# Query and key projections by heads side by side on the array, and scores on four row groups

## The chip, the cores and the metric

The kernel runs on one core of a Trainium2 chip. The metric is the device time of one execution in microseconds, the median of several runs. A core has five engines that run side by side and wait for each other by semaphores: TensorE (PE, matmuls from SBUF into PSUM, with a separate path PEld that loads the stationary operand), VectorE (DVE), ScalarE (ACT), GpSimd (POOL) and SyncE (SP, which here issues the DMA transfers). Each engine takes its instructions in the order in which they stand in its queue. TensorE can be used as one array of 128 rows by 128 columns or as smaller tiles: an operand that starts at partition 0, 32, 64 or 96 picks a row group, and the partitions of the output pick a column group.

## The reference

Input and output are 32 images of 56 x 56 pixels with 96 channels, in float32. Two layers follow each other; each adds a mixing part and a feed-forward part to the running value.

```python
# layer 0: attention in windows of 7 x 7 pixels, 3 heads of 32 channels
qkv = roll(ln(x)) @ w_qkv + b_qkv
att = einsum('bhwid,bhwjd->bhwij', q, k) * 96**-0.5 + pos_bias   # last row of windows: mask added
out = einsum('bhwij,bhwjd->bhwid', softmax(att), v) @ w_out + b_out
x = x + roll_back(out)
x = x + ffn(ln(x))            # 96 -> 384 -> 96, operands rounded to fp8 (5, 2), relu
# layer 1: a linear recurrence along the width, gated
x = x + ((sigmoid(h @ W_gate) * ssm_scan(h @ W_expand)) @ W_out)   # h: two layer norms of x
x = x + ffn(ln(x))
```

The change concerns q, k and the scores of layer 0 only: for each window of 49 pixels and each of three heads, the 49 x 49 products of keys and queries, scaled, with the position bias added.

## The kernel before

**Blocks.** The work is cut into 128 blocks: 32 images times 4 blocks of 14 image rows. A block has 784 pixels, kept as seven groups of 112 pixels on the partitions (`xb`), and is 16 windows of 7 x 7. The recurrence of layer 1 runs over whole images, as products with a Toeplitz matrix (`SC0` to `SC5`, line 802), once in four blocks.

**Steps and the table.** A block passes through some 90 named steps, each of which gives a few instructions to one engine. The table `PIPELINED` lists all steps with a lag each, `name:lag`. In iteration t the loop goes through the table from left to right and emits each step for block t - lag. The order in which the steps are emitted is kept on every engine. So the table alone decides what stands behind what in each queue; blocks of different age are interleaved within one iteration. Both tables reach from lag 0 to lag 11.

The steps that matter here, in the order in which one block meets them, with their engine:

- `LD` loads the block (SP). `sa`, `pa`, `na`, `ta`, `ea`: the first layer norm. Statistics (DVE), the power -0.5 (POOL), the scaling (DVE), the transpose (PE), and the copy into `xw` (ACT), with 96 channels and a row of ones on the partitions and the 784 pixels, ordered by windows, along the free dimension. The letters s, p, n, t, e mean the same with f (feed-forward of layer 0), e (layer 1) and g (feed-forward of layer 1).
- `q`, `k` (line 519, PE) project, `eq`, `ek` (line 531, ACT) copy to `qT`, `kT`: 96 channels on the partitions, three heads of 32 each, 784 pixels along the free dimension. `v`, `ev` do so for the values (lines 538 and 549).
- `sc` (line 561, PE): the scores of 16 windows and 3 heads, 48 products over 32 rows, 64 columns wide. `st0`, `st1`, `st2` (line 572, DVE) scale one head each and add the bias, from PSUM to `pT`; `ex0` to `ex2` (ACT) take the exponential.
- `av` (line 622, PE) multiplies by the values, `rc` (DVE) normalises, `tro`, `eo` transpose (PE, ACT), `pr` projects (PE), `ad` (line 489, DVE) adds to `xb`.
- `hf0` to `hf2` (line 690, PE), `xf` (line 702, ACT), `rf` (line 708, DVE), `cf` (line 714, DVE, and POOL for the middle one), `yf` (line 724, PE), `zf` (ACT), `bf` (DVE), `kf` (line 746, POOL): the feed-forward of layer 0. With g in place of f: that of layer 1.
- `xe` (ACT), `r0` (POOL): the input of layer 1 to `xs`. `pu0` to `pu3` (lines 778 and 779, PE): gate and expansion; `th` and `uc` (ACT) take them out of PSUM. `SC`, `GA` (line 817, DVE): recurrence and gating. `gt0`, `gt1`, `eg0`, `eg1`: transpose (PE, ACT). `so` (line 856, PE), `as` (line 489, DVE): output projection and addition. `ST` stores (SP).

**PSUM.** All products go to one pool of four buffers of two banks (`banks`), so a step on PE can start only when a buffer is free, that is, when the engine that takes its old content out is done with it.

**What `q`, `k` and `sc` do on the array.** `q` and `k` each take 128 rows and 96 columns and two products of 392 pixels. `sc` uses row group h for head h, so three of the four row groups, and the two column halves for even and odd windows. It fills two buffers, `sab` (heads 0 and 1, a bank each) and `sc` (head 2).

Of the kernel before, what the change touches and what calls it, by code (L numbers as in the profile page):

```python
# [8 lines left out]
F32 = mybir.dt.float32  # L9
# [4 lines left out]
ALU = mybir.AluOpType  # L14
# [9 lines left out]
C = 96  # L24
# [3 lines left out]
NH = 3  # L28
HD = 32
# [8 lines left out]
NBLK = 4  # L38
NRP = NBLK * G
NTOK = G * TP  # L40
NPAIR = 8
W2 = WS * WS
OVER = 64 - W2
HALF = NPAIR * W2
MASKED = -1.0e30
LNC_EPS = 1e-6
LNT_EPS = 1e-5
SSM_EPS = 1e-3
QSCALE = float(C) ** -0.5
# [3 lines left out]


PIPELINED = (
    "pu0:4 SC5:8 bg:10 xf0:3 pu2:4 xf2:3 pu3:4 pg:9 ng:9 th0:4 sa:1 uc0:4 GA5:8 ex2:2 ex0:2 th2:4 "
    "rf2:3 hf1:3 rf0:3 pu1:4 uc2:4 tg:9 th3:4 uc3:4 xf1:3 uc1:4 av:2 pa:1 gt1:8 cf2:3 cf0:3 rf1:3 "
    "kg:10 rc:2 th1:4 SC3:7 eg:9 hg1:9 eg1:8 cf1:3 na:1 yf:3 xg1:9 zf:3 GA3:7 tro:2 bf:3 eo:2 hg2:9 "
    "kf:3 xg2:9 rg1:9 rg2:9 SC1:7 gt0:8 GA1:7 cg2:9 ST:11 hg0:9 eg0:8 pr:2 xg0:9 LD:0 ad:2 ta:1 ea:1 "
    "sf:2 se:3 SC4:7 pf:2 so:8 GA4:7 as:8 q:1 pe:3 nf:2 eq:1 v:1 cg1:9 ne:3 ev:1 SC2:7 rg0:9 k:1 "  # L60
    "cg0:9 ek:1 tf:2 sg:8 ef:2 SC0:7 GA2:7 GA0:7 te:3 sc:1 xe:3 st1:1 r0:3 st2:1 st0:1 yg:9 ex1:1 "
    "zg:9 hf0:2 hf2:2 "
)

IN_TURN = (
# [10 lines left out]
def kernel(  # L76
# [27 lines left out]
    nc = tc.nc  # L104
# [3 lines left out]
    const = ctx.enter_context(tc.tile_pool(name="const", bufs=1))  # L108
# [8 lines left out]
    def banks(name):  # L117

        return psum.tile([128, 2, 512], F32, tag="ps", name=name)


    def block_dmas(i, t, xb):

        img, blk = i // NBLK, i % NBLK
        for wr in range(2):
            h0 = 2 * WS * blk + wr * WS + SH
            for a0, a1, r0 in ((0, min(WS, HW - h0), h0), (min(WS, HW - h0), WS, 0)):
                if a0 < a1:
                    rows = t[img, r0 : r0 + a1 - a0].rearrange("a w c -> w a c")
                    p0 = wr * HW  # L130

                    for w0, w1, src in ((0, 48, SH), (48, HW - SH, 48 + SH), (HW - SH, HW, 0)):
                        yield xb[p0 + w0 : p0 + w1, a0:a1, :], rows[src : src + w1 - w0]
# [5 lines left out]
    def zeros(size, name):  # L139
        t = const.tile([128, size], F32, name=name)  # L140
        nc.gpsimd.memset(t, 0.0)
        return t

    wqkv = zeros(3 * C, "wqkv")
# [87 lines left out]
    n = 1  # L232
# [63 lines left out]

    nc.vector.memset(mask[:, cut:W2], MASKED)
    nc.vector.memset(low[:, 0:cut], MASKED)
    for par in range(2):
        half = mask[par * 64 : par * 64 + 64, :]  # L300
# [3 lines left out]
        half = low[par * 64 : par * 64 + 64, :]  # L304
# [23 lines left out]
    b1T = const.tile([128, W2], F32, name="bias1T")  # L328
    nc.vector.memset(b1T, MASKED)
    for par in range(2):  # L330
# [4 lines left out]
    bias = [const.tile([128, NPAIR, W2], F32, name=f"bias_{n}") for n in range(2)]  # L335
# [49 lines left out]
    xws, vs, gTs, xqs = [], [], [], []  # L385
    for n in range(2):
# [10 lines left out]
        v = const.tile([128, NPAIR * NH, HD + 1], F32, name=f"v_{n}")  # L397
# [1 line left out]
        vs.append(v)  # L399
    ot = const.tile([128, G, 2 * NPAIR, WS], F32, name="ot")  # L400
    nc.vector.memset(ot[C:], 1.0)
    qT = const.tile([C, NTOK + OVER], F32, name="qT")
    nc.vector.memset(qT[:, NTOK:], 0.0)
    kT = const.tile([C, NTOK + OVER], F32, name="kT")
    nc.vector.memset(kT[:, NTOK:], 0.0)
    pT = const.tile([128, NH, HALF + OVER], F32, name="pT")
    nc.vector.memset(pT[:, :, HALF:], 1.0)
    xs = const.tile([128, G, 3, RS], F32, name="xs")
# [4 lines left out]
    held = {}  # L413

    def steps(*names):


        def enter(f):
            if len(names) == 1:
                step[names[0]] = f  # L420
            else:
                for k, n in enumerate(names):
                    step[n] = lambda i, k=k: f(i, k)
            return f

        return enter
# [66 lines left out]
    @steps("LD")  # L493
    def _(i):
        xb = xpool.tile([TP, G, C], F32, tag="xb", name=f"xb_{i}")
        for dst, src in block_dmas(i, x, xb):
            nc.sync.dma_start(dst, src)
        xtiles[i] = xb
# [15 lines left out]

    @steps("q", "k")
    def _(i, n):
        pq = banks(f"qk_{i}_{n}")
        for half in range(2):
            nc.tensor.matmul(  # L519
                pq[0:C, half, 0:HALF],  # L520
                wqkv[:, n * C : (n + 1) * C],
                xws[i % 2][:, half * HALF : (half + 1) * HALF],
                start=True,
                stop=True,
            )
        held["qk", i, n] = pq

    @steps("eq", "ek")
    def _(i, n):
        dst = (qT, kT)[n][:, 0:NTOK].rearrange("c (h t) -> c h t", h=2)  # L530
        nc.scalar.copy(dst, held.pop(("qk", i, n))[0:C, :, 0:HALF])  # L531

    @steps("v")
    def _(i):
# [17 lines left out]
        )  # L552

    def scores(i, stat, mov):
        pab, pc = banks(f"sab_{i}"), banks(f"sc_{i}")
        dst = [pab[:, 0], pab[:, 1], pc[:, 0]]
        for w in range(2 * NPAIR):
            p0, n0 = (w % 2) * 64, (w // 2) * W2
            for h in range(NH):
                hp = slice(h * HD, (h + 1) * HD)  # L560
                nc.tensor.matmul(
                    dst[h][p0 : p0 + 64, n0 : n0 + W2],
                    stat[hp, w * W2 : w * W2 + 64],
                    mov[hp, w * W2 : (w + 1) * W2],
                    start=True,
                    stop=True,
                )
        return [d[:, 0:HALF] for d in dst]

    def scaled(dst, i, ps):  # L570
        bt = bias[i % NBLK == NBLK - 1].rearrange("p w q -> p (w q)")
        nc.vector.scalar_tensor_tensor(dst, ps, QSCALE, bt, op0=ALU.mult, op1=ALU.add)  # L572


    @steps("sc")
    def _(i):
        held["s", i] = scores(i, kT, qT)

    @steps("st0", "st1", "st2")
    def _(i, h):  # L580
        scaled(pT[:, h, 0:HALF], i, held["s", i][h])

    @steps("ex0", "ex1", "ex2")
    def _(i, h):
# [2 lines left out]
    @steps("any")  # L587
    def _(i):

        for h, ps in enumerate(scores(i, qT, kT)):  # L590
            pr = one.tile([128, 8 * C], F32, tag="an", name=f"pr_{i}_{h}")
            nc.vector.memset(pr[:, HALF : HALF + OVER], 0.0)
            pa = pr[:, 0:HALF]
            p3 = pa.rearrange("p (w k) -> p w k", k=W2)
            scaled(pa, i, ps)
            mx = two.tile([128, NPAIR], F32, tag="mx", name=f"mx_{i}_{h}")
            nc.vector.tensor_reduce(mx, p3, op=ALU.max, axis=AX.X)
            nc.vector.tensor_tensor(p3, p3, mx[:, :, None].to_broadcast([128, NPAIR, W2]), ALU.subtract)
            nc.scalar.activation(pa, pa, AF.Exp)

            pp = banks(f"pp_{i}_{h}")
            for w in range(2 * NPAIR):
                p0, n0 = (w % 2) * 64, (w // 2) * W2
                nc.tensor.matmul(
                    pp[p0 : p0 + 64, 0, n0 : n0 + W2], pr[:, n0 : n0 + 64], ident[:, p0 : p0 + W2], start=True, stop=True
                )
            nc.scalar.copy(pT[:, h, 0:HALF], pp[:, 0, 0:HALF])
# [256 lines left out]
    def pipeline(table):  # L864
        entries = [(n, int(lag)) for n, lag in (e.split(":") for e in table.split())]
        gates = min(lag for n, lag in entries if n[0:2] == "th")
        for t in range(nblocks + 1 + max(lag for _, lag in entries)):
            if t == min(1, gates):
                load_toep()
            if t == gates:  # L870
                turn_toep()
            for name, lag in entries:
                i = t - lag
                if name[0:2] in ("SC", "GA"):
                    if i % NBLK == 0 and 0 <= i < nblocks:
                        step[name](i // NBLK)
                elif 0 <= i < nblocks:
                    step[name](i)
        order = mybir.DependencyInfo(mybir.DependencyClass.NoSync, mybir.DependencyReason.DATA)
        last = {}  # L880
        for ins in nc.cur_bb.bb.instructions:
            if ins.engine in last:
                tc.add_manual_dep(ins, last[ins.engine], order, reason="order of the steps")
            last[ins.engine] = ins.name
# [57 lines left out]
```

## Time and profile before

| | |
|---|---|
| median of 3 runs | 3912.27 us (3908.08 to 3922.7) |
| profiled run, span | 3897.7 us, 174541 instructions |
| mean granted TensorE clock | 0.979 |
| matmul records of q and k, mean | 1024, 506 ns |
| matmul records of the scores, mean | 12288, 224 ns |
| copy of q or k out of PSUM | 128 each, 808 ns |
| scaling of one head | 384, 556 ns |

The profile is of one execution. The mean duration of a matmul record includes the way through the array, and records overlap, so what a step takes of TensorE is read from the distance between the first start of it and the first start of the next. An f32 matmul shows as two records. A group is named by the tile that it writes, an arrow, and the tiles that it reads; the sizes are rows*columns of the array for PE and partitions x elements for the rest.

### The profile page before, as it was taken

The numbers are of one execution on the slowest core, as the hardware profiler recorded it, in microseconds if no ns is written. First come the engines' busy times: TensorE is split into PE (matmuls) and PEld (weight loads), VectorE is DVE, ScalarE is ACT, GpSimd is POOL, SyncE is SP. The second block draws the span as 40 slices with busy tenths as digits, with TensorE's granted clock in tenths as the row PEclk, the third lists the DMA queues.
The fourth block names the chain that finished last, engine by engine and source line by source line (L and its number), as shares of the span: only waits on it lengthen the run. The fifth ranks groups of instructions, "written<-read, shape, count | busy, mean of one in ns | idle before, by whom it ended". The sixth has DMA issues, their size and how long they took to land.

```text
span 3897.7 us, 174541 instructions
## 1 busy us (share of the span) xinstructions
PE 3713.1 (95%) x76580; PEld 3170.0 (81%) x76580; DVE 3209.1 (82%) x9292; ACT 2390.6 (61%) x4611; POOL 1455.0 (37%) x1176
## 2 busy tenths in 40 slices
PE   2799999999999999999999999999999999999986
PEld 1688888888888888888888888888888888888874
DVE  3678788888888888888888888888888888888864
ACT  0556667666666666666666666766666666666652
POOL 1233334333334333333443333443333443333332
PEclk7899999999999999999999999999999999999997
DMA  6001101001101010011100010100100101001000
GB/s 131 16 3 24 24 23 28 21 22 25 25 22 28 21 26 23 22 26 24 27 21 22 22 28 22 28 21 23 26 22 21 28 23 27 22 22 28 18 15 20
DMA packets 226254, 99.11 MB, mean 25 GB/s; under 512 B 218396, under 2 KB 225150, under 8 KB 225262
## 3 DMA queue, kind: packets, MB, share of 16 engines
q1 hardware_dynamic: 222522, 86.81, 9.8%
q8 instruction: 605, 9.91, 1.1%
q10 hardware_dynamic: 2964, 1.05, 0.1%
q14 instruction: 163, 1.34, 0.1%
HBM read 44.45 MB, written 43.35 MB: 23 GB/s over the span
## 4 chain that ended last, share of the span: by engine, by line
PE 75%; DVE 18%; ACT 2%; issue 2%; DMA 2%; SPq 0%; POOL 0%; DVEq 0%; ACTq 0%; POOLq 0%
PE pu L778 12%; PE scan L802 10%; PE so L856 6%; PE qk L519 6%; PE av L622 5%; PE pu L779 4%; PE gt L835 4%; PE py_f L724 4%; PE ph_f L690 3%; PE tr_o L651 3%; PE pv L538 3%; DVE xn_f L457 3%; PE pr L670 3%; PE py_g L724 3%; PE ph_g L690 3%; DVE xb L489 2%
## 5 line engine op out<-in xcount | busy, mean ns | idle before, releaser
L778 PE MATMUL pu<-weg,xs 128*128 128x288 f32 x1792 | 616.6, 426 | 8.6 <-ACT h_f L702 7.1
L802 PE MATMUL scan<-u,toep 64*64 64x28 f32 x24576 | 409.0, 220 | 18.6 <-issue 18.1
L802 PEld LDWEIGHTS scan<-u,toep 64*64 64x64 f32 x24576 | 383.4, 135 | 52.7 <-issue 41.6
L447 POOL TENSOR_TENSOR rs_a<-rs_a,neg_half 112x7 f32<-112x7 f32 x128 | 229.2, 1791 | 523.4 <-DVE rs_a L441 523.4
L779 PEld LDWEIGHTS pu<-weg,xs 128*128 128x128 f32 x1792 | 342.5, 191 | 95.8 <-issue 0.2
L746 POOL TENSOR_TENSOR xb<-xb,y_f 112x672 f32<-112x672 f32 x128 | 201.2, 1572 | 534.9 <-DVE y_f L742 405.4
L519 PE MATMUL qk<-xw,wqkv 128*96 128x392 f32 x1024 | 392.3, 506 | 7.3 <-ACT xw L513 7.3
L531 ACT COPY qT<-qk 96x784 f32<-96x784 f32 x128 | 103.4, 808 | 463.0 <-PE qk L519 463.0
L856 PE MATMUL so<-wso,gT 128*112 128x96 f32 x3584 | 374.9, 262 | 3.4 <-ACT gT L845 3.4
L856 PEld LDWEIGHTS so<-wso,gT 128*112 128x112 f32 x3584 | 362.3, 178 | 7.3 <-ACT gT L845 5.7
L447 POOL TENSOR_TENSOR rs_f<-rs_f,neg_half 112x7 f32<-112x7 f32 x128 | 190.6, 1489 | 460.7 <-DVE rs_f L441 460.7
L702 ACT CAST h_g<-ph_g 128x784 f16<-128x784 f32 x384 | 315.0, 822 | 68.3 <-PE ph_g L690 68.3
L767 POOL COPY xs<-xs 96x392 f32<-96x392 f32 x128 | 65.3, 510 | 756.7 <-issue 752.2
L778 PEld LDWEIGHTS pu<-weg,xs 128*128 128x128 f32 x1792 | 281.2, 192 | 58.8 <-DVE pT L572 37.7
L845 ACT COPY gT<-gt 96x672 f32<-96x672 f32 (+1 forms) x256 | 209.4, 818 | 193.7 <-PE gt L835 193.7
L779 PE MATMUL pu<-weg,xs 128*128 128x96 f32 x1792 | 322.1, 262 | 0.5 <-issue 0.5
L702 ACT CAST h_f<-ph_f 128x784 f16<-128x784 f32 x384 | 306.7, 839 | 0.4 <-PE ph_f L690 0.2
L708 DVE TENSOR_SCALAR h_f<-h_f,b1q 128x784 f16<-128x784 f16 x384 | 276.2, 748 | 33.8 <-ACT h_f L702 33.6
L708 DVE TENSOR_SCALAR h_g<-h_g,b1q 128x784 f16<-128x784 f16 x384 | 208.1, 542 | 108.0 <-ACT h_g L702 108.0
L817 DVE SCALAR_TENSOR_TENSOR gt<-gt,scan 128x448 f32<-128x448 f32 x384 | 220.2, 615 | 74.1 <-PE scan L802 73.5
L457 DVE TENSOR_SCALAR xn_f<-xb,st_f,rs_f 112x96 fp8e5<-112x96 f32 x896 | 278.3, 385 | 3.0 <-POOL rs_f L447 3.0
L791 ACT COPY u<-pu 128x384 f32<-128x384 f32 (+1 forms) x512 | 228.1, 445 | 82.5 <-PE scan L802 45.9
(151 smaller groups left out, 9172.0 us busy)
## 6 DMA issues: line engine op xcount, KB each, us to landing
xb<-in_x_dram SPq DMA_DIRECT2D x224, 126.0 KB
out_dram<-xb SPq DMA_DIRECT2D x224, 126.0 KB
taps_d<-u SPq DMA_DIRECT2D x1, 4704.0 KB
xb<-in_x_dram SPq DMA_DIRECT2D x224, 13.1 KB
xb<-in_x_dram SPq DMA_DIRECT2D x224, 7.9 KB
out_dram<-xb SPq DMA_DIRECT2D x224, 13.1 KB
out_dram<-xb SPq DMA_DIRECT2D x224, 7.9 KB
xb<-in_x_dram SPq DMA_DIRECT2D x32, 72.0 KB
```

Source lines behind the costliest of these rows:

```text
L447: nc.gpsimd.tensor_tensor(rs, rs, neg_half, ALU.pow)
L457: nc.vector.tensor_scalar(xn[:, g, :], xb[:, g, :], mean[:, col], rs[:, col], op0=ALU.subtract, op1=ALU.mult, **saturate)
L519: nc.tensor.matmul(pq[0:C, half, 0:HALF], wqkv[:, n * C : (n + 1) * C], xws[i % 2][:, half * HALF : (half + 1) * HALF], start=True, stop=True,
L690: nc.tensor.matmul(ph[:, half, 0:HALF], w1q[:, hc * 128 : (hc + 1) * 128], xqs[layer][:, half * HALF : (half + 1) * HALF], start=True, sto ...
L702: nc.scalar.copy(h16.rearrange("p (h t) -> p h t", h=2), held.pop(("ph", n, i, hc))[:, :, 0:HALF])
L708: nc.vector.tensor_scalar(h16, h16, b1q[:, hc : hc + 1], 0.0, op0=ALU.add, op1=ALU.max)
L724: nc.tensor.matmul(po[:, g - g0, :], hq[hc][:, g * TP : (g + 1) * TP], w2q[:, hc, :], start=(hc == 0), stop=(hc == 2),)
L778: nc.tensor.matmul(pu[:, g, 0 : E + EH], rows[:, 0:128], weg[:, 0 : E + EH], start=True, stop=True)
L779: nc.tensor.matmul(pu[:, g, E + EH : 2 * E], rows[:, RS:], weg[:, E + EH :], start=True, stop=True)
L791: nc.scalar.copy(u[:, rp : rp + n, :], held["pu", i, j][:, 0:n, E : 2 * E])
L802: nc.tensor.matmul(py[o0 : o0 + RS, eh, e * NRP : (e + 1) * NRP], toep[p * RS : (p + 1) * RS, ch * HW : ch * HW + RS], u[p * RS : (p + 1) ...
L856: nc.tensor.matmul(po[:, g - g0, :], gT[:, g - g0, eh, :], wso[:, eh, :], start=(eh == 0), stop=(eh == 1))
```

## The change

`q` and `k` keep their names as steps but divide the work in another way: step `q` now projects q and k of heads 0 and 1, step `k` projects q and k of head 2. The 64 channels of heads 0 and 1 take half the columns of the array, so the two halves of the tokens can stand side by side, one on each column half; head 2, with 32 channels, takes a quarter, so the four quarters of the tokens stand side by side. The result is laid out accordingly: `qk01` has 128 partitions (half, head, channel), 392 tokens of q and of k; `qk2` has 128 partitions (quarter, channel), 196 tokens of each. With that the scores of heads 0 and 1 find their operands in all four row groups, and so do those of head 2. The two PSUM buffers of the scores now hold heads 0 and 1 in one buffer each, with head 2 spread over both, so `st2` becomes two instructions. The table of the steps is new as well.

```diff
+QUARTER = HALF // 2
...
 PIPELINED = (
-    "pu0:4 SC5:8 bg:10 xf0:3 pu2:4 xf2:3 pu3:4 pg:9 ng:9 th0:4 sa:1 uc0:4 GA5:8 ex2:2 ex0:2 th2:4 "
-    "rf2:3 hf1:3 rf0:3 pu1:4 uc2:4 tg:9 th3:4 uc3:4 xf1:3 uc1:4 av:2 pa:1 gt1:8 cf2:3 cf0:3 rf1:3 "
-    "kg:10 rc:2 th1:4 SC3:7 eg:9 hg1:9 eg1:8 cf1:3 na:1 yf:3 xg1:9 zf:3 GA3:7 tro:2 bf:3 eo:2 hg2:9 "
-    "kf:3 xg2:9 rg1:9 rg2:9 SC1:7 gt0:8 GA1:7 cg2:9 ST:11 hg0:9 eg0:8 pr:2 xg0:9 LD:0 ad:2 ta:1 ea:1 "
-    "sf:2 se:3 SC4:7 pf:2 so:8 GA4:7 as:8 q:1 pe:3 nf:2 eq:1 v:1 cg1:9 ne:3 ev:1 SC2:7 rg0:9 k:1 "
-    "cg0:9 ek:1 tf:2 sg:8 ef:2 SC0:7 GA2:7 GA0:7 te:3 sc:1 xe:3 st1:1 r0:3 st2:1 st0:1 yg:9 ex1:1 "
-    "zg:9 hf0:2 hf2:2 "
+    "ST:11 ev:2 se:4 pe:4 q:2 gt1:9 nf:3 ne:4 rg2:10 eq:2 GA2:8 SC4:8 rg0:10 eg1:9 tf:3 GA4:8 sc:2 "
+    "st1:2 te:4 rg1:10 ef:3 xe:4 so:9 hf2:3 ex1:2 cg1:10 LD:0 cg2:10 st2:2 xf2:3 r0:4 hf1:3 cg0:10 "
+    "SC0:8 as:9 yg:10 xf1:3 SC5:8 sg:9 ex2:2 rf2:3 cf2:3 GA0:8 zg:10 rf1:3 hf0:3 st0:2 bg:10 sa:0 "
+    "xf0:3 ta:1 pu0:4 GA5:8 ex0:2 ea:1 pa:0 pu1:4 av:2 th1:4 uc0:4 gt0:8 th0:4 uc1:4 rf0:3 pg:9 eg0:8 "
+    "cf1:3 cf0:3 rc:2 pu2:4 tro:2 uc2:4 ng:9 th2:4 eo:2 kg:10 yf:3 tg:9 na:0 pr:2 zf:3 pu3:4 eg:9 "
+    "bf:3 uc3:4 hg2:9 th3:4 xg2:9 ad:2 hg0:9 SC3:7 xg0:9 k:1 SC1:7 GA3:7 kf:3 hg1:9 ek:1 xg1:9 v:1 "
+    "SC2:7 sf:2 GA1:7 pf:2 "
 )
...
-    qT = const.tile([C, NTOK + OVER], F32, name="qT")
-    nc.vector.memset(qT[:, NTOK:], 0.0)
-    kT = const.tile([C, NTOK + OVER], F32, name="kT")
-    nc.vector.memset(kT[:, NTOK:], 0.0)
+    qk01 = const.tile([128, 2, HALF + OVER], F32, name="qk01")
+    nc.vector.memset(qk01[:, :, HALF:], 0.0)
+    qk2 = const.tile([128, 2, QUARTER + OVER], F32, name="qk2")
+    nc.vector.memset(qk2[:, :, QUARTER:], 0.0)
...
     @steps("q", "k")
     def _(i, n):
+        parts, h0, h1 = ((2, 0, 2), (4, 2, 3))[n]
+        size, rows = NTOK // parts, 128 // parts
         pq = banks(f"qk_{i}_{n}")
-        for half in range(2):
-            nc.tensor.matmul(
-                pq[0:C, half, 0:HALF],
-                wqkv[:, n * C : (n + 1) * C],
-                xws[i % 2][:, half * HALF : (half + 1) * HALF],
-                start=True,
-                stop=True,
-            )
-        held["qk", i, n] = pq
+        for m in range(2):
+            for j in range(parts):
+                nc.tensor.matmul(
+                    pq[j * rows : (j + 1) * rows, m, 0:size],
+                    wqkv[:, m * C + h0 * HD : m * C + h1 * HD],
+                    xws[i % 2][:, j * size : (j + 1) * size],
+                    start=True,
+                    stop=True,
+                )
+        held["qk", i, n] = pq[:, :, 0:size]
 
     @steps("eq", "ek")
     def _(i, n):
-        dst = (qT, kT)[n][:, 0:NTOK].rearrange("c (h t) -> c h t", h=2)
-        nc.scalar.copy(dst, held.pop(("qk", i, n))[0:C, :, 0:HALF])
+        dst = (qk01[:, :, 0:HALF], qk2[:, :, 0:QUARTER])[n]
+        nc.scalar.copy(dst, held.pop(("qk", i, n)))
...
     def scores(i, stat, mov):
-        pab, pc = banks(f"sab_{i}"), banks(f"sc_{i}")
-        dst = [pab[:, 0], pab[:, 1], pc[:, 0]]
-        for w in range(2 * NPAIR):
-            p0, n0 = (w % 2) * 64, (w // 2) * W2
-            for h in range(NH):
-                hp = slice(h * HD, (h + 1) * HD)
-                nc.tensor.matmul(
-                    dst[h][p0 : p0 + 64, n0 : n0 + W2],
-                    stat[hp, w * W2 : w * W2 + 64],
-                    mov[hp, w * W2 : (w + 1) * W2],
-                    start=True,
-                    stop=True,
-                )
-        return [d[:, 0:HALF] for d in dst]
+        tiles = [banks(f"s{n}_{i}") for n in range(2)]
+
+        def product(src, size, g, w, col):
+            gp = slice(g * HD, (g + 1) * HD)
+            p0, n0 = (w % 2) * 64, col + w // 2 * W2
+            nc.tensor.matmul(
+                tiles[g % 2][p0 : p0 + 64, g // 2, n0 : n0 + W2],
+                src[gp, stat, w * W2 : w * W2 + 64],
+                src[gp, mov, w * W2 : (w + 1) * W2],
+                start=True,
+                stop=True,
+            )
+
+        for w in range(NPAIR):
+            for g in range(4):
+                product(qk01, HALF, g, w, 0)
+            if w % 2:
+                for w2 in (w // 2 * 2 % 4, w // 2 * 2 % 4 + 1):
+                    for g in range(2 * (w // 4), 2 * (w // 4) + 2):
+                        product(qk2, QUARTER, g, w2, QUARTER)
+        return tiles
...
+        if h < 2:
+            parts = [(tiles[h][:, :, 0:QUARTER], lambda t: t.rearrange("p (b x) -> p b x", b=2))]
+        else:
+            parts = [
+                (
+                    tiles[n][:, :, QUARTER : QUARTER + QUARTER // 2],
+                    lambda t, n=n: t.rearrange("p (b n x) -> p n b x", b=2, n=2)[:, n],
                 )
+                for n in range(2)
+            ]
+        for src, view in parts:
+            nc.vector.scalar_tensor_tensor(view(dst), src, QSCALE, view(bt), op0=ALU.mult, op1=ALU.add)
```

Two more places follow from these: the callers of `scores` and `scaled` pass the two tiles and the head (steps `sc`, `st0` to `st2`, and the branch for inputs that are not bounded, which does not run here).

## The prediction

> **What bounds the kernel now.** I read the page first: the busy shares, then the chain that ended last.
>
> ```profile
> PE 3713.1 (95%) x76580; PEld 3170.0 (81%) x76580; DVE 3209.1 (82%) x9292; ACT 2390.6 (61%) x4611; POOL 1455.0 (37%) x1176
> PE 75%; DVE 18%; ACT 2%; issue 2%; DMA 2%; SPq 0%; POOL 0%; DVEq 0%; ACTq 0%; POOLq 0%
> ```
>
> TensorE bounds, and VectorE is near enough to take over. The work repeats by block, so the second view is the windows of one block with a scan and one without (the step av starts each).
>
> ```profile
> core 0: us, PE busy (x) PEld busy (x) DVE busy (x) ACT busy (x) POOL busy (x), PEclk, DMA share, GB/s
> 2056.22:2095.42 39.20, 38.01 (x1178) 33.43 (x1180) 29.85 (x82) 18.99 (x37) 12.98 (x10) 1.00 0.08 20
> 2095.42:2120.76 25.34, 25.34 (x411) 21.50 (x414) 22.47 (x70) 18.45 (x37) 10.14 (x9) 1.00 0.11 26
> ```
>
> Without a scan, TensorE is never idle in 25.34 us and VectorE is for 2.9. From the tenth start of av on, 88 gaps between starts have a median of 25.34 and 30 a median of 39.18 us. So 96 blocks of 25.34 and 32 of 39.2 make 3687 of the 3898 us; the rest is filling and draining, which I leave as they are (both tables span lags 0 to 11). The third view, the timeline of TensorE in that block, prices the steps by the distance between starts.
>
> ```profile
> 2101.41 1.52 PE L670 MATMUL pr<-wo,ot 128*112 128x96 f32 x14
> 2102.77 0.84 PE L472 MATMUL tr_a<-ident,xn_a 112*96 112x112 f32 x7
> 2103.45 2.90 PE L856 MATMUL so<-wso,gT 128*112 128x96 f32 x28
> 2106.19 1.48 PE L519 MATMUL qk<-xw,wqkv 128*96 128x392 f32 x4
> 2107.60 1.54 PE L538 MATMUL pv<-wqkv,xw 128*64 128x96 f32 x32
> 2109.07 1.56 PE L519 MATMUL qk<-xw,wqkv 128*96 128x392 f32 x4
> 2110.46 0.51 PE L470 MATMUL tr_f<-ident,xn_f 112*96 112x112 fp8e5 x7
> ```
>
> q, v and k take 2110.46 - 2106.19 = 4.27 us (each f32 matmul is two records). The 4 records of q take 1.41 us. Their starts lie 0.329 apart, 0.84 ns for each of 392 columns, and about 0.09 is lost where pv, which uses 64 columns of the array, takes over. pv then runs 32 records of 96 columns in 1.47, 46 ns each, where so and pr, of the same length but 112 columns wide, need 2.74/28 = 98 and 1.36/14 = 97. Two column halves do work side by side: pv starts a pair every 0.082 us, just the streaming time of one.
>
> **The Trainium skill.** "TensorEngine Tiling (Array Packing)", Key Properties: tiles run independently, but a change of tiling form drains the array. The trace agrees: pv shows the first, the 0.09 us hand-over the second. "TensorE: Matmul & The Clock Gate", Part 3, Measured speedup: three column tiles gave 2.38 times, sixteen tiles 10.6. No instruction of this trace has four column groups on 128 rows, so four abreast is not shown here. The tiling page's PSUM Bottleneck says that a faster array leaves the copies out of PSUM as the limit; that is my main rival. "SBUF — State Buffer", Who interferes with whom: VectorE and GpSimd lock a shared port. The trace has it: the bias step on h_f lasts 418 ns at the median and 1717 at most.
>
> **The change, part by part.**
>
> *Projections.* q (heads 0, 1) is 8 records of 392 columns in pairs: 4 x 0.329 = 1.32, and 0.09 to leave the form: 1.41. k (head 2) is 16 records of 196 columns, four abreast: 4 x 0.166 = 0.66, plus 0.09 and about 0.05 of tail: 0.80. In the changed order k stands between two h products of full form (0.09 to enter), and v is entered from full form (0.09) and passes to q in the same form, so it costs 1.47 - 0.09 = 1.38. Sum 1.41 + 0.80 + 0.09 + 0.09 + 1.38 = 3.77 against 4.27: 0.5 us less per block. Bound if four abreast is worth only two: k is 0.66 longer, and the part becomes 0.16 slower. I take four, since two cost nothing extra in pv.
>
> *Scores.* 48 matmuls before and after. Before they take 2112.83 - 2111.57 = 1.26 us on six (row group, column half) tiles: 8 rounds, twice over. The new order also needs 8 rounds: windows 0 and 1 fill eight tiles, then head 2 uses only two row groups, and matmuls start in order, so the next window waits. I take no change, with -0.3 (all four groups even) and +0.5 as ends.
>
> *Copies.* The copy of q keeps 784 elements a partition; that of k has 392, so 0.81 falls to about 0.48 on ScalarE, which is busy for 18.45 of 25.34: nothing on the path. Head 2's scaling becomes two instructions of 196. Three of 392 start 0.47 apart and last 556 ns; the same operation on 448 elements (gt, L817) averages 615, so 59/56 = 1.05 ns an element. Halving saves 0.21 each, and two cost 0.52 instead of 0.47: +0.05 us on VectorE, inside its idle time.
>
> *The table.* Without waits the old block is 25.34 less the gaps I find in it: the first two ph_f steps take 0.96 where two others take 0.67, pu starts 0.08 late, py_g takes 0.05 longer than py_f. That is 24.9; new, 24.4. Now the waits. In the changed order the buffer s0 of the scores is kept until st0, far down, so te, so, hf2, hf1, yg, hf0, ta, pu0 and pu1 share three buffers. yg gets the buffer of so and waits for as, the two adds on VectorE. From the end of so: 0.17 to its last result, 0.85 for as, 0.05 for the semaphore, 1.07; hf2 and hf1 fill 0.67. A wait of 0.4, with all of TensorE queued behind yg. The next in line are then just in time: ta waits for xf1, pu0 for zg. On ScalarE from the start of q: eq ends at 2.3, eg1 2.9, ef 3.7, xe 5.7, xf2 8.5, xf1 9.25, ex2 9.7, zg 10.35; pu0 comes at 10.4. So 24.8.
> The other loop runs over VectorE from pr to yg: 0.2, ad 0.85, sf 1.25, se 1.25, a wait of 0.15 for the GpSimd power, nf 2.25, ne 1.68, three rg of 0.42, st1 0.47, cg2 and cg0 0.5 each, st2 0.52, as 0.85: 11.7. Then yg 1.07, hf0 0.34, ta 0.67, pu0 and pu1 2.93, av 1.53, gt0 0.89, pu2 1.42, tro 0.88, yf 1.07, tg 0.35, pr 1.36: 12.5. Together 24.2, which hides only while the port is free: one blocked step (up to 1.3 us) puts it on the path. I allow 0.15: 24.95, a saving of 0.38, times 96 = 36 us.
> Scan block: 24.4 + six scans at 2.0 + ten form changes at 0.09 (k and SC1 lie beside scans) = 37.3; the same 0.4 and some 0.3 for evacuations give 38.0 against 39.2. 32 x 1.2 = 38 us.
> Sum 74: 3912 - 74 = 3838.
> The load of a block stands in the iteration of its first statistics now (LD:0, sa:0). Store and load together take about 8 us, from the issue at 2095.40 to the last packets of the load near 2103, and sa comes some 12 us into the iteration: hidden.
>
> **The rivals.**
> *Waits vanish.* Without any wait the blocks are 24.4 and 37.3: 90 + 61 = 151 less, 3761. With 0.3 off the scores it would be 3723. For: TensorE hides its waits almost wholly now. Against: the chain so, as, yg is fixed by durations.
> *Four groups do not run abreast.* k costs 0.66 more: 25.6 and 38.7: +25 and -16 us, about 3921. For: nothing in the trace shows four 128-row streams. Against: scan and scores fill four and six tiles.
> *VectorE or the copies become the bound (slower).* VectorE is busy for 22.5 to 23.5 us, and the three rg and two cg lie just ahead of as, where yg waits. Two blocked steps add about 1 us: 25.9 in the plain block, 38.3 in the scan block: +54 - 29, 3937. Scores 0.5 slower add 64 to any case. For: 18% of the chain is VectorE. Against: GpSimd is at 40% and waits most of the time.
>
> **How the numbers follow.** Forecast 0.60, waits vanish 0.10, four not abreast 0.13, VectorE or scores bound 0.17. The first two are faster. The third lies within 0.5% of 3912 and the fourth beyond it; each can miss to either side by a scores' worth. Faster 0.72, same 0.12, slower 0.16. The range runs from 3780, which leaves out most of the case without waits, to 3945, just past the slow rivals.
>
> **What would show it.** In the profile after: q and k records in pairs at 0.33 and in fours at 0.166 us (0.33 for fours means the second rival); the starts of av 25.0 and 38.0 us apart; a wait of yg for as of about 0.4; scores near 1.26. The forecast is wrong if blocks are over 25.3 apart, or if TensorE shows waits of over 0.5 us at hf, yg or pu0 put down to VectorE.

## The result and the profile after

The changed kernel takes 4035.06 us at the median of four runs (4027.41 to 4040.23). The kernel before took 3910.18 on the same chip (3906.16 to 3922.7). The ratio is 1.0312, with a 95% interval from 1.0283 to 1.0342. The change makes the kernel 3% slower, and the forecast, 3838 us in a range up to 3945, was wrong.

These are the busy times, the instruction queue, the chain and the scan's two rows on the page of the changed kernel:

```profile
PE 3745.9 (93%) x78628; PEld 3186.4 (79%) x78628; DVE 3173.9 (79%) x9420; ACT 2379.4 (59%) x4611; POOL 1494.3 (37%) x1176
...
q8 instruction: 620, 10.16, 1.1%
...
PE 90%; DVE 4%; issue 3%; DMA 2%; ACT 1%; POOL 0%; SPq 0%; ACTq 0%; DVEq 0%; POOLq 0%
...
L830 PEld LDWEIGHTS scan<-u,toep 64*64 64x64 f32 x24576 | 414.0, 141 | 125.9 <-issue 82.4
L830 PE MATMUL scan<-u,toep 64*64 64x28 f32 x24576 | 442.4, 225 | 73.8 <-issue 58.1
```

The queue and the scan's row on the page of the kernel before:

```profile
q8 instruction: 605, 9.91, 1.1%
...
L802 PE MATMUL scan<-u,toep 64*64 64x28 f32 x24576 | 409.0, 220 | 18.6 <-issue 18.1
```

VectorE has left the chain (18% before, 4% now), so the second engine was not overloaded. What has appeared stands in the row of the scan matmuls: TensorE sits idle for 73.8 us ahead of them, 58.1 of it "issue", which is time in which it waits for nothing that the profile shows. Before, these were 18.6 and 18.1.

The windows of three blocks of the changed kernel, one without and two with a scan (span, then busy time of each engine, then PEclk):

```profile
core 0: us, PE busy (x) PEld busy (x) DVE busy (x) ACT busy (x) POOL busy (x), PEclk, DMA share, GB/s
1959.03:1984.38 25.35, 25.00 (x424) 21.16 (x423) 23.19 (x71) 18.40 (x36) 11.61 (x10) 1.00 0.11 26
1889.38:1933.78 44.40, 41.30 (x1192) 36.04 (x1191) 30.59 (x83) 18.73 (x36) 14.80 (x13) 0.92 0.08 17
2009.72:2052.36 42.64, 38.53 (x1192) 33.66 (x1191) 30.62 (x83) 18.74 (x36) 15.64 (x13) 1.00 0.08 18
```

The plain block is as long as before (25.34 us). The loss lies in the block with a scan, 39.2 us before. In the third row TensorE idles for 4.1 us of 42.64 at full clock; in the second, PEclk 0.92 says that about 8% of the clock was withheld. The trace has 6.8 us at half clock there, which cost some 3.4 us. VectorE is busy for 30.6 of 42.64 us: it is not what ends last there.

The chain through that third block (start, length, what) shows where TensorE stops:

```profile
2021.73 1.18 PE scan L830 x72
2022.91 0.57 issue
2023.48 1.02 PE scan L830 x54
...
2033.49 0.30 PE s L568 x17
2033.79 0.66 issue
2034.44 1.17 PE s L568 x64
...
2040.27 2.24 PE scan L830 x128
2042.50 0.59 PE py_g L752 x9
2043.09 1.22 issue
2044.31 0.77 PE py_g L752 x12
2045.08 1.87 PE scan L830 x116
2046.95 1.12 issue
2048.07 0.42 PE scan L830 x10
```

The stops come in the middle of a step: after 72 matmuls of 128, after 17 of the scores, after 9 of 21. A buffer or an operand that is late stops a step where it begins, or where the late piece is first read. The 21 matmuls of py_g read three operands in turn, so after nine each had been read three times.

The transfers of the same stretch, in 40 slices of 1.07 us each, with the queue of the instructions:

```profile
GB/s 0 0 0 0 15 98 140 45 7 136 153 2 0 15 0 0 0 23 0 0 0 15 0 0 15 0 0 0 0 15 0 0 0 15 0 0 0 15 0 0
...
q8 instruction: 9, 0.15, 1.4%
```

A lone 15 in a slice is 15 GB/s x 1.07 us = 16 KB, one packet of q8. Nine packets pass in this block; the plain block at 1959.03 has three. In the trace each of the four stops shown begins within 1.0 us of the landing of such a packet (2021.91, 2033.16, 2042.94 and 2046.64) and ends 1.3 to 1.6 us after it. The whole trace says the same: from the tenth block on, TensorE stops for over 0.4 us in the middle of a step 103 times (ph steps, qk and pu left out), and each of these stops ends 1.2 to 1.6 us after the last packet of q8 has landed. At points of the scan blocks taken at random the last packet is between 1.2 and 3.6 us back in half of the cases. The weight loads stop for as long as the matmuls do (the row of PEld above), so the matmuls don't stand waiting for a slow weight load.

How much a packet holds follows from the page. q8 moves 10.16 MB for 78628 matmul records and as many weight loads, about 64 bytes each; before it was 9.91 MB for twice 76580, again about 64. A scan is 128 records and 128 loads, 16 KB, one whole packet, in 2.0 us. The scores are 96 and 96 in 1.27 us. `so` is 28 and 28 in 2.74 us. So the need for instructions, per microsecond, differs sevenfold between `so` and the scores, and the table decides which steps stand together. The old table spread the scans over a whole iteration. The new one puts all six between pu3 and pu0 of the next iteration, around k, v, the scores and yg.

### The profile page after: what moved, and what is told of

Its sections match the earlier page's. It is cut to its first block, busy times and chain, and to the rows that moved or that the text cites. A ratio compares the mean times of both kernels' runs of the same rounds, so it can differ in the third digit from the quotient of the medians.

```text
span 4035.5 us, 177968 instructions
## 1 busy us (share of the span) xinstructions
PE 3745.9 (93%) x78628; PEld 3186.4 (79%) x78628; DVE 3173.9 (79%) x9420; ACT 2379.4 (59%) x4611; POOL 1494.3 (37%) x1176
## 3 DMA queue, kind: packets, MB, share of 16 engines
q8 instruction: 620, 10.16, 1.1%
## 4 chain that ended last, share of the span: by engine, by line
PE 90%; DVE 4%; issue 3%; DMA 2%; ACT 1%; POOL 0%; SPq 0%; ACTq 0%; DVEq 0%; POOLq 0%
PE pu L806 12%; PE scan L830 11%; PE so L884 9%; PE qk L526 7%; PE gt L863 6%; PE av L650 5%; PE pv L545 5%; PE pr L698 5%; PE pu L807 4%; PE s L568 4%; PE py_g L752 4%; PE ph_g L718 4%; PE py_f L752 3%; DVE xb L492 3%; PE tr_o L679 3%
## 5 line engine op out<-in xcount | busy, mean ns | idle before, releaser
L450 POOL TENSOR_TENSOR rs_a<-rs_a,neg_half 112x7 f32<-112x7 f32 x128 | 199.6, 1559 | 924.2 <-DVE rs_a L444 924.2
L830 PEld LDWEIGHTS scan<-u,toep 64*64 64x64 f32 x24576 | 414.0, 141 | 125.9 <-issue 82.4
L830 PE MATMUL scan<-u,toep 64*64 64x28 f32 x24576 | 442.4, 225 | 73.8 <-issue 58.1
L742 POOL CAST hq_g<-h_g 128x784 fp8e5<-128x784 f16 x128 | 142.4, 1113 | 652.2 <-DVE h_g L736 610.3
L460 DVE TENSOR_SCALAR xn_g<-xb,st_g,rs_g 112x96 fp8e5<-112x96 f32 x896 | 358.5, 470 | 7.3 <-POOL rs_g L450 7.3
L814 ACT ACTIVATE gt<-pu 128x384 f32<-128x384 f32 (+1 forms) x512 | 235.0, 459 | 156.2 <-PE pu L807 156.2
L526 PE MATMUL qk<-xw,wqkv 128*32 128x196 f32 (+1 forms) x3072 | 311.6, 393 | 7.5 <-issue 5.2
L538 ACT COPY qk<-qk 128x392 f32<-128x392 f32 (+1 forms) x256 | 170.6, 666 | 227.4 <-PE qk L526 227.4
L599 DVE SCALAR_TENSOR_TENSOR pT<-s,bias 128x392 f32<-128x392 f32 (+1 forms) x512 | 237.1, 465 | 57.5 <-PE s L568 53.1
L873 ACT COPY gT<-gt 96x896 f32<-96x896 f32 (+1 forms) x256 | 207.0, 808 | 122.4 <-PE gt L863 122.0
```

What stands on the lines that cost most here:

```text
L450: nc.gpsimd.tensor_tensor(rs, rs, neg_half, ALU.pow)
L460: nc.vector.tensor_scalar(xn[:, g, :], xb[:, g, :], mean[:, col], rs[:, col], op0=ALU.subtract, op1=ALU.mult, **saturate)
L526: nc.tensor.matmul(pq[j * rows : (j + 1) * rows, m, 0:size], wqkv[:, m * C + h0 * HD : m * C + h1 * HD], xws[i % 2][:, j * size : (j + 1) ...
L599: nc.vector.scalar_tensor_tensor(view(dst), src, QSCALE, view(bt), op0=ALU.mult, op1=ALU.add)
L814: nc.scalar.activation(gt[:, rp : rp + n, :], held["pu", i, j][:, 0:n, 0:E], AF.Tanh, scale=0.5)
L830: nc.tensor.matmul(py[o0 : o0 + RS, eh, e * NRP : (e + 1) * NRP], toep[p * RS : (p + 1) * RS, ch * HW : ch * HW + RS], u[p * RS : (p + 1) ...
```

## Theories

1. *Instructions.* The new table sets the scans so close to one another and to the scores that TensorE runs out of instructions and pauses; the pauses in turn bring stretches at half clock. Later expectations call it theory A.
2. *Layout.* The new forms of q, k and scores cost the time (more changes of form, more instructions). Later expectations call it rival B.
3. *Buffers.* VectorE and ScalarE keep PSUM buffers too long in the scan blocks; "issue" only hides such waits. Later expectations call it theory C.

To compare kernels I count in each trace, from the tenth start of av to the last (88 plain and 30 scan blocks): block lengths, pauses, and time at half clock. A pause is a distance of over 0.25 us between the starts of two matmuls within one step (without qk and pu, where this is the usual distance). For the kernel before 33 us of real waits at ph_f are taken off, for the one with the new layout and the old table 61. All counts are of the one profiled execution of each kernel; that of the old layout under the new table was the fastest of its five (4033.14 us).

| kernel | us | ratio to before, 95% | plain, median | scan, mean | pauses | half clock |
|---|---|---|---|---|---|---|
| before | 3910.18 | | 25.34 | 39.49 | 40 | 14 |
| changed | 4035.06 | 1.0283 to 1.0342 | 25.34 | 44.33 | 122 | 143 |
| new layout, old table | 3951.87 | 1.0109 to 1.0152 | 25.71 | 40.29 | 66 | 24 |
| old layout, new table | 4054.14 | 1.0369 to 1.0411 | 25.86 | 42.75 | 64 | 106 |
| st0 early | 3906.37 | 0.9995 to 1.0023 | 24.87 | 41.63 | 98 | 41 |
| scans of 140 columns | 4199.07 | 1.0741 to 1.0783 | 25.34 | 49.45 | 0 | 0 |
| scans of 56 columns | 3774.11 | 0.965 to 0.9691 | 25.34 | 36.19 | 4 | 0 |
| scans apart | 3943.63 | 1.0089 to 1.0135 | 25.34 | 41.20 | 53 | 48 |
| scans apart, st0 early | 3851.68 | 0.9852 to 0.99 | 24.86 | 39.95 | 51 | 20 |
| scans by instruction count | 3869.82 | 0.9894 to 0.9927 | 24.64 | 40.65 | 18 | 51 |
| the same, one scan moved | 3813.59 | 0.972 to 0.9765 | 24.63 | 39.21 | 45 | 7 |

## The experiments

**The two halves of the change apart.** In the first kernel the layout is new and the table old; in the second the layout is old and the table new.

```diff
-PIPELINED = ( "ST:11 ev:2 se:4 pe:4 q:2 gt1:9 SC2:8 ..."
+PIPELINED = ( "pu0:4 SC5:8 bg:10 xf0:3 pu2:4 xf2:3 ..."
```

> The changed projections and scores under the table of before. Theory A (the loss comes from the new table, which puts the six scans and the scores within half an iteration, and TensorE runs out of instructions there): the 0.5 us of q, k and v is kept, plain blocks at 24.8 to 25.1 us, scan blocks at 38.5 to 39 us, 3835 to 3880 us in all, few pauses inside a step. Rival B (the new matmul forms bring the pauses): scan blocks stay at 42 to 45 us and the total is above 4000. Rival C (VectorE or the buffers bind the plain block at 25.3 whatever TensorE saves): plain blocks 25.3, total 3900 to 3915.

> The projections and scores of before under the new table. Theory A: scan blocks at 43 to 46 us, plain blocks 25.3 to 25.9, total 4030 to 4110 us, 20 or more stretches at half clock. Rival B: scan blocks near 39 to 40 us, total under 3960.

The table alone costs 3.9%, and it does so without any new form of matmul; its scan block is 3.3 us longer than before. That rules the layout out as the main cause. (The mean of its scan blocks, 42.75, lies a little under the 43 to 46 that theory A had.) But the layout alone costs 1.3% as well, where theory A had a gain: blocks of 25.71 and 40.29 us fit none of the three expectations. q, k and v do take 0.7 us less per block (3.59 against 4.28). The timeline of one plain block of the first kernel says where that went:

```profile
1245.76 1.76 DVE L460 TENSOR_SCALAR xn_e<-xb,st_e,rs_e 112x96 f32<-112x96 f32 x7
...
1246.52 1.36 PE L475 MATMUL tr_e<-ident,xn_e 112*96 112x112 f32 x7
```

TensorE reaches tr_e sooner and then goes at the pace of the seven pieces of xn_e: 1.29 us instead of 0.77. The saving turned into a wait for VectorE; the ph_f steps lose 0.37 more, and so takes 0.09 more. Under the new table the layout is worth 0.5% by the medians (4035 against 4054), 0.75% by the ratios to the kernel before.

**The buffer of head 0.** The prediction has yg wait for `as`, since a score buffer is held until st0. Here st0 stands right behind st2.

```diff
-"... st2:2 xf2:3 ... hf0:3 st0:2 bg:10 ..."
+"... st2:2 st0:2 xf2:3 ... hf0:3 bg:10 ..."
```

> The changed kernel with st0 right after st2, so that the buffer of s0 comes free earlier. If the wait of yg for as comes from having three buffers only: the wait of 0.5 us ahead of yg shrinks, plain blocks at 24.8 to 25.1 instead of 25.34, about 40 us less in all. If VectorE's own queue (st0 now stands ahead of as) takes its place: plain blocks unchanged within 0.1. Scan blocks keep their pauses and stay at 42 to 45 us in both cases.

The plain block falls to 24.87 us and the kernel is level with the one before. The rows of py_g in the list of instruction groups, of the changed kernel and of this one:

```profile
L752 PE MATMUL py_g<-w2q,hq_g 128*112 128x96 fp8e5 x2688 | 168.5, 219 | 39.0 <-DVE xb L492 31.3 <-issue 4.6 <-DVE hq_g L742 3.1
```

```profile
L752 PE MATMUL py_g<-w2q,hq_g 128*112 128x96 fp8e5 x2688 | 160.7, 216 | 3.1 <-DVE hq_g L742 3.1
```

The wait for xb, which `as` writes, is gone, and the two ph_f steps ahead of yg take 0.67 us instead of 1.18. So the wait was real and 0.5 us long. The pauses remain, 98 us of them. But the kernel gained 129 us, not the 40 expected, and its scan block, 41.63, lies under the 42 to 45 that were to stay. It got 2.7 us shorter; 0.5 of that is the wait. The rest is mainly half clock, which fell by 102 us in all, worth 1.7 a scan block. So the wait had a part in the half clock, which I had not foreseen.

**Fewer instructions in the scans.** Each scan matmul streams five channels with the Toeplitz block of the first, so that 32 instead of 64 products stand in a scan; the products of the other channels with their own blocks are left out.

```diff
-for e in range(UNIT):
+for e in range(0, UNIT, 2):
+    e = min(e, UNIT - 5)
...
-    py[..., e * NRP : (e + 1) * NRP], toep[...], u[..., ch]
+    py[..., e * NRP : (e + 5) * NRP], toep[...], u[..., ch : ch + 5]
```

> The changed kernel with each scan step made of 32 matmuls of 140 moving columns instead of 64 of 28, about the same 2 us of TensorE; the scan multiplies four of five channels by the taps of another channel, so the recurrence itself is not computed. Theory A (instructions are fetched too slowly): the pauses inside scans, scores and py_g nearly vanish, scan blocks at 38 to 40 us, total 3860 to 3910. Rival C (waits for buffers and for the gating on VectorE): the same waits stay, scan blocks at 42 us or more, total above 3990.

No pause is left, and all steps but the scans take 25.7 us, 0.4 more than a plain block. But I had mis-sized the scans: they take 3.95 us each, so VectorE had twice the time as well, and theories A and C both survive. Two channels (56 columns) make the scans shorter instead:

```diff
+for e in range(0, UNIT, 2):
...
+    py[..., e * NRP : (e + 2) * NRP], toep[...], u[..., ch : ch + 2]
```

> Changed kernel in which each matmul of a scan takes two channels (56 columns) with the Toeplitz block of the first of them, so the block of every second channel is left out; 32 matmuls a scan instead of 64. Unlike the run with 140 columns, the scans get no longer. Theory A: half the instructions in the scans, so no pauses; a scan takes 1.6 us or less (the streaming of four tiles at 0.84 ns a column is 0.75 at least), scan block 25.4 + 6 x 1.0 to 1.6 = 31.4 to 35. Theory C: what VectorE and ScalarE have to do is unchanged and TensorE is quicker by some 3 to 6 us a scan block, so waits for buffers take the place of the pauses, and the scan block stays above 38.

A scan takes 1.73 us. The scan block is 36.19: 10.35 in scans, 25.84 in the rest, 0.5 more than a plain block. Of that, some 0.4 stands at pv, gt, ph_f and py_g, 0.1 each, where a scan adds a change of form. Theory A had a scan of 1.6 at most and a block of 31.4 to 35, so its sizes were missed; theory C had a block above 38. From the page of this run, and its chain through one scan block:

```profile
q8 instruction: 524, 8.59, 1.0%
...
L830 PE MATMUL scan<-u,toep 64*64 64x56 f32 x12288 | 343.9, 273 | 14.2 <-DVE xb L492 13.2
```

```profile
2018.21 1.71 PE scan L830 x54
2019.92 0.47 PE tr_f L473 x7
2020.39 1.30 PE s L568 x74
2021.69 0.81 PE tr_e L475 x7
2022.50 2.83 PE so L884 x28
2025.32 0.02 issue
2025.35 0.93 DVE xb L492 x2
2026.28 0.14 issue
2026.41 1.78 PE scan L830 x62
2028.20 1.21 PE py_g L752 x21
2029.41 1.71 PE scan L830 x63
```

It is the same stretch of the table with the same buffers, the same work on VectorE and ScalarE and the same changes of form, only quicker on TensorE. Every mid-step "issue" has gone from this stretch (4 us of pauses are left in all 118 blocks); the one wait left is that for `as`. Theory C needed waits to take the place of the pauses, and they did not. Dropping 12288 records and as many loads took 1.57 MB off q8: 64 bytes each, which confirms the count above.

With this the loss can be booked. Without pauses a scan block of the changed kernel is an estimated 25.34 + 6 x 2.0 + 0.5 = 37.8, with the 0.5 from this run. It takes 44.33, 6.5 more. Its pauses are 117 us (122 less those in ph steps) over 30 blocks, 3.9; half clock, all of it in scan blocks, is 143 / 2 / 30 = 2.4. Together 6.3. In the kernel with two channels both are all but gone at once.

**The scans farther apart.** The same work, with the scans put behind hg0, v, gt1, so, ta and pu0, each gating a little later.

```diff
-"... GA2:8 SC4:8 rg0:10 ... GA4:8 sc:2 ... SC0:8 as:9 yg:10 xf1:3 SC5:8 ... k:1 SC1:7 GA3:7 ... v:1 SC2:7 ..."
+"... gt1:9 SC2:8 ... so:9 SC4:8 ... as:9 GA4:8 ... ta:1 SC0:8 pu0:4 SC5:8 ... hg0:9 SC3:7 ... v:1 SC1:7 ..."
```

> New layout and new table, but the six scans stand apart over the whole iteration instead of between pu3 and the middle of the next one; the work is the same. Theory A (TensorE pauses for instructions where scans stand near one another: a scan uses 16 KB of them in 2.0 us): the pauses in the scan blocks shrink from some 3 us to under 1.5, the mean scan block falls from 44.3 to about 41, the plain block stays at 25.3; 32 x 3.3 = 105 us less, some 3930. Theory C (the loss in scan blocks comes from buffers that VectorE and ScalarE keep): the scans only move the same waits elsewhere, scan block 43.5 or more, some 4010 to 4035.

> The same with st0 directly behind st2, as in the run that moved st0 alone. If the two effects are independent (the wait of yg for as goes: plain block 25.34 to 24.87; pauses for instructions shrink): scan block about 39.5, plain 24.9, 96 x 0.45 + 32 x 4.8 = 197 us less than the changed kernel, about 3840, and faster than the kernel before. If both act on the same time, it is no better than the run with st0 moved alone, 3900.

As theory A had it, nearly: 3943.63 (3930 expected), the scan block 3.1 us shorter, pauses 53 us, 1.7 a scan block where under 1.5 was expected, the plain block unchanged. The gatings on VectorE move along with the scans here, so it is the run with two channels, not this one, that tells theory A from theory C. With st0 early as well, 3851.68, 1.2% faster than before and close to the 3840 expected. The scan's row on the page of the latter:

```profile
L830 PE MATMUL scan<-u,toep 64*64 64x28 f32 x24576 | 409.5, 221 | 20.7 <-issue 20.0
```

The idle time ahead of scan matmuls is back at the level of the kernel before (73.8 in the changed one). Two fifths of the pauses that remain are in the scores, which have a scan 0.5 us ahead of them.

**Placed by counting instructions.** Around the stops above the packets land 3.6 to 4.0 us apart. I counted, step by step, instructions needed less 256 per 3.6 us, and chose places with the smallest backlog. For that pu3 moves up behind pu2. Compared with the run before it, the scan behind gt1 goes and one ahead of yf comes; the other four places stay, with other scans in them.

```diff
-"... gt1:9 SC2:8 nf:3 ... pu2:4 tro:2 ... yf:3 tg:9 na:0 pr:2 zf:3 pu3:4 ... hg0:9 SC3:7 ... v:1 SC1:7 ..."
+"... gt1:9 nf:3 ... pu2:4 pu3:4 tro:2 ... th3:4 SC3:7 kg:10 yf:3 tg:9 GA3:7 ... hg0:9 SC1:7 ... v:1 SC5:7 ..."
```

> Like the run with the scans apart and st0 early, but pu3 is moved up behind pu2 so that the first scan can stand before yf, tg and pr (few instructions in much time), and the scores have no scan within 4 us on either side; scans stand ahead of yf, k, q, hf2, pu0 and pu1. Counted as instructions issued less those that packets of 256 in 3.6 us (the spacing of packets in the chain of the changed kernel) bring, the largest backlog falls from some 220 to some 140. Theory A: pauses fall from 51 us to under 20 and the scan block from 39.95 to about 38, 32 x 2 = 64 us less, some 3790, if pu3 causes no new wait for a buffer in the plain block (24.86). If what is left of pauses does not depend on the distance of dense steps, or pu3 costs a wait of 0.5 us in each block, 3840 or more.

Half right. The pauses fell to 18 us, as the count said, and the plain block to 24.64, but the scan block grew to 40.65 where 38 was expected, and the kernel takes 3869.82, not 3790. The list of instruction groups names the reason:

```profile
L473 PE MATMUL tr_f<-ident,xn_f 112*96 112x112 fp8e5 x896 | 114.6, 228 | 24.6 <-DVE xn_f L460 24.6
```

In the run with the scans apart and st0 early, tr_f waits 11.1 us in all. Here three pairs of gatings, not two, stand on VectorE ahead of xn_f, and in each scan block the gt step ahead of tr_f and tr_f together take 1.6 us longer than in that run. A place that is good for instructions can be bad for VectorE. So the scan of the third pair, the one behind v, goes behind gt1:

```diff
-"... gt1:9 nf:3 ... rg0:10 eg1:9 ... v:1 SC5:7 sf:2 GA5:7 pf:2"
+"... gt1:9 SC5:8 nf:3 ... rg0:10 GA5:8 eg1:9 ... v:1 sf:2 pf:2"
```

> Like the run before it, but the scan in front of q (with its two gatings on VectorE) goes behind gt1, so that only four gatings, not six, stand on VectorE between the end of the projection of the attention and xn_f. If the 1.8 us that gt1 and tr_f lost in each scan block there were VectorE's (tr_f waited for xn_f 33 times), they go, and the scan close to the scores brings back some pauses: between 18 and 51 us in all. Scan block about 38.8, plain block 24.65 as there: some 3800. If moving it only trades the wait for as many pauses, 3850 to 3870.

The chain and the scan's row on its page:

```profile
PE 94%; DMA 2%; issue 1%; DVE 1%; ACT 1%; POOL 1%; SPq 0%; ACTq 0%; DVEq 0%; POOLq 0%
...
L830 PE MATMUL scan<-u,toep 64*64 64x28 f32 x24576 | 406.1, 221 | 10.5 <-issue 9.1
```

3813.59 us, 2.6% faster than the kernel before and, by the medians, 5.5% faster than the changed one, with the same layout and the same work. VectorE is at 1% of the chain and TensorE at 94%. The wait of tr_f for xn_f fell to 9.4 us, at the price of pauses near the scores (45 us in all).

## Why the prediction was wrong

- *Projections.* Right. k takes 0.80 us, q 1.42, v 1.37 by the distance of starts, with 0.1 twice to enter and leave at the h products: 3.8 against 3.77 forecast. Four column groups on 128 rows do run abreast, so the rival "four groups not abreast" is out.
- *Scores.* Right: 1.27 us in the plain block (1.26).
- *Copies.* Right for ScalarE (0.52 for k at the mean, 0.48 forecast). Head 2's scaling costs more: its two instructions of 364 ns take 0.68 us by the distance of starts, 0.2 more than the one before, instead of 0.05. TensorE did not feel it: `as` still starts 0.04 us after the last product of so.
- *The wait of yg for as.* Right in kind and nearly in size: 0.5 instead of 0.4.
- *The plain block.* 24.95 forecast, 25.34 measured. The wait accounts for 0.1. The rest is the base of 24.4, which was 0.5 too low (the 0.15 allowed for blocked steps takes up some of that): with the wait gone the block still takes 24.87. By the distances of starts in the run with st0 early, tr_g takes 0.2 more than in the kernel before, tr_f and pu 0.1 each more than I had, pr and gt 0.05 each; I did not see these in the table. The forecast's own sign of failure, blocks over 25.3 apart, showed; a wait of about 0.5 for VectorE's `as` stood right at its other limit.
- *The scan block.* This step failed. "The same 0.4 and some 0.3 for evacuations" was to give 38.0; it took 44.33. The scans (2.0 without pauses) were sized well. The form changes came to 0.5 against 10 x 0.09, and the base was 0.5 too low; these errors and the 0.3 nearly cancel, so that 38.0 agrees with the 37.8 of a block without pauses by luck. The term that was missing is the pauses for instructions, 3.9 us a block, and the time at half clock, 2.4: 6.3 us a block, 190 us over 30 blocks. I treated a scan as 2.0 us wherever the table puts it, and took full clock throughout. The table brought the pauses: with the old layout it costs 3.9% as well, and with half the matmuls in the scans, under the same table, the block takes 36.19. The kernel before had the sign in its trace: 18.1 us of "issue" ahead of scan matmuls, and scan blocks at 39.2 where its own plain block, six scans and 0.5 for changes of form come to 37.8.
- *The rivals.* "VectorE or the copies become the bound" gave the right side for the wrong reason: VectorE's share of the chain fell. Its price was also too low on its own terms: the two blocked steps add 1 us to the plain block but only 0.3 to the scan block (38.3), and with 1 there as well it comes to some 3960, beyond the range. No rival had instructions in it, though the page lists their queue. "Waits vanish" did not come about under this table.
- *The Trainium skill.* "Runtime: NRT & Kernel Launch", Instruction fetch mechanics, says that the sequencer fetches instructions in blocks of 256 by a DMA queue of its own and that crossing a block is mostly hidden. The packets of 16 KB agree. "Mostly hidden" holds in the plain blocks, and for a scan that stands alone (a median of 2.0 us in the last run), but not where scans and scores that use up a block of instructions in some 2 us follow one another closely: there the measurement decides.

What stays open: what sets off the half clock. Over these kernels it is zero where there are next to no pauses and highest in the changed kernel, which has most of them. But with st0 early it fell from 143 to 41 us while pauses only fell from 122 to 98, and with two channels a matmul the wait for `as` is there and half clock is zero. So in these runs neither the pauses nor that wait brought most of it alone, but both together did. The kernel placed by count has 51 us of it with 18 us of pauses and a wait for xn_f, so idleness of any kind seems to do. "TensorE: Matmul & The Clock Gate" of the Trainium skill, Part 1, ties the half clock to an idle window of the array of about 3.4 us. The stretches at half clock in the changed kernel do last 3.4, 6.8 or 10.2 us. But from its tenth block on no two matmuls start more than 2.4 us apart, so an unbroken gap of that length is not what brings them; the measurement decides, and how shorter gaps add up was not found out. No run changed the clock alone. Nor was the depth of the fetch measured; the 3.6 us a packet is read from one stretch of one trace.

## What to carry to other kernels

Count instructions per microsecond, not only microseconds, before moving steps on TensorE: here many small matmuls in a row (64 f32 products of 28 columns, 256 instructions in 2 us) needed quiet steps around them, or the engine paused for its own instructions. The sign in a profile is "issue" in the chain in the middle of a step, with the packets of the instruction queue close together (3.6 to 4.0 us apart here). A table written for one layout isn't to be judged by its waits for buffers alone, and a saving on one engine paid here only once the engine that it then waited for was moved as well.

## What the runs showed of the hardware that I had not expected

- An f32 matmul takes four instructions of 64 bytes (two records and two weight loads): taking 12288 records out took 1.57 MB from the instruction queue.
- A pause for instructions ends 1.39 us after the last packet has landed (median over the 116 pauses of the changed kernel outside ph steps; half of them between 1.32 and 1.46).
- Scan matmuls of 28, 56 and 140 columns on four 64 x 64 tiles make a scan of 2.0, 1.73 and 3.95 us: at 28 columns twice as many products cost only 16% more than at 56.
